# Four graph layers on one core: layer 2's sums, norms and gathers written out in a fixed order

## The chip, the core and the metric

The kernel runs on one core of a Trainium2 chip. The core has four compute engines that work side by side, each through its own queue of instructions: TensorE (PE in the profile; its weight loads are listed as PEld), VectorE (DVE), ScalarE (ACT) and GpSimd (POOL). SyncE (SP) issues DMA transfers; POOL issues the gathers, which are indirect DMAs. Engines wait for one another through semaphores. SBUF is the on-chip memory; PSUM holds the results of matmuls, in eight banks of 512 float32 per partition.

The metric is the device time of one execution, in microseconds (us). The kernel before took 2139.83 us, the median of three runs (2136.4 to 2140.26).

## What is computed

The input `x` holds 8 graphs (batches) of 2048 nodes with 64 features each, and one symmetric adjacency matrix `adj` with about 0.4% ones. Four layers follow, each of the form `x = layernorm(x + gnn(x, adj))`. The change concerns layer 2, and what layer 3 needs at its start. Layer 2 reads, cut to what matters:

```python
agg = jnp.einsum('ij,bjf->bif', A, x) / jnp.maximum(deg, 1.0)[None, :, None]
out = jax.nn.relu(x @ W_self + b_self + agg @ W_neigh + b_neigh)
out = (out - mean(out)) * rsqrt(var(out) + eps) * ln_gamma + ln_beta      # over the 64 features
x   = layernorm(x + out)
```

Layer 3 is attention with four heads: scores `h_n · h_m` with `h = x Wh` per head, a softmax over a node's neighbours, a mean of `h`, an output matrix `Wo`, and a second attention round. The kernel uses `x_n (Wh^T Wh) x_m` for the score, so for each head it keeps `G = Wh^T Wh`, and transposed copies of `Wh` and `Wo` (`AT`, `WoT`). The exponents are shifted by a number per head that comes from the mean score of node tile 0's nodes with themselves.

## The kernel before

Nodes are cut into 16 tiles of 128 (one node per partition); a tile holds 8 batches × 64 features = 512 float32 per partition. `X` (SBUF) is the current `x`.

**Layer 3's weights.** Ahead of layer 2 (lines 649 to 672) a loop over the four heads loads blocks `wb` and `ob` by SP, subtracts one column on DVE, makes `G` with one matmul, and transposes `wb` and `ob` on TensorE, with three DVE copies from PSUM.

**Layer 2, first part** (lines 742 to 760, the loop over `turns`). Per tile: transpose `X`, multiply by both weight matrices (L747), copy the neighbour part `y` to SBUF and to the DRAM table `ytab`, and split it into three bf16 pieces `Y` (hi, mid, lo: L753, L758, L759); the self part with its biases becomes `S` (L754); `b2`, layer 2's beta, is added to `X` in advance (L760).

**Layer 2, second part** (lines 762 to 835). The sum over neighbours is made in two ways. Tiles 0 to 8 are *dense*: 16 steps of 3 matmuls each (L828) over `ET`, the adjacency in fp8, and the three pieces of `Y`. Tiles 15 down to 9 go *by list*: for each of three slots POOL issues four gathers of rows of `ytab` (`fetch`, L186), and four matmuls of 32 columns (L814, with a 0/1 selection matrix copied by ACT at L810) add them up. Such a group of one tile and slot is called a quad here; there are 21. They are spread over the dense steps by `LATE` and `EARLY`, and the gathers run two quads ahead.

`finish` (L775) follows a tile's sum:

```python
STT zf = zf * r_deg + S          # L779, DVE, in PSUM
Relu on zf                       # L780, ACT, in PSUM
layer_norm(zs)                   # DVE L137-L143, ACT L151
z *= g2 ; X = z + X              # L786, L787, DVE
layer_norm(X)                    # DVE, ACT L151
Xo = X ; xtab row block <- Xo    # L792 ACT, L793 SP
```

A norm is four `bn_stats` (L137), a chain of twelve small DVE instructions for one over the root of the variance (L121 to L143, a Newton iteration), and eight activations on ACT per tile, one per batch, with scale and bias from an SBUF column (L151). `mates` joins two tiles in one PSUM tile of two banks (three such buffers) and norms them together: 9 groups, so 18 of these chains. A PSUM tile stays occupied until both tiles' z has been added to `X`.

After tile 0's norm, `first_nodes` transposes its rows (`turn_nodes`, copy by ACT), makes its scores with itself for four heads (L701 on TensorE, L703 on DVE), the shifts (L705 to L710), and the products of its nodes with `G` (`side`, L687 to L693).

**What orders the work.** In layer 2 the framework's scheduler picks each engine's order from priorities and its own estimates. Layer 3's loop is in a `manual_schedule`: there each engine takes its instructions in the order in which the program writes them. Layer 3 gathers rows of `xtab`, all of which must be written first.

Of the kernel before, what the change touches and what calls it, by code (L numbers as in the profile page):

```python
# [21 lines left out]
F32 = mybir.dt.float32  # L22
# [5 lines left out]
AF = mybir.ActivationFunctionType  # L28
ALU = mybir.AluOpType
# [3 lines left out]
P = 128  # L33
# [7 lines left out]
LEVEL = 15.0  # L41
# [7 lines left out]
def kernel(ctx: ExitStack, tc: tile.TileContext, ins: dict, out: bass.AP):  # L49
# [30 lines left out]
    def rows(name, src, pool):  # L80

        n = src.shape[0]
        t = pool.tile([P, n], F32, name=name)
        nc.sync.dma_start(t, src.unsqueeze(0).to_broadcast([P, n]))
        return t
# [556 lines left out]
    def misc(shape):  # L642
        return ps_m.tile(shape, F32, name="pm")

    ones_x = [hp.tile([P, B, D], F32, name=f"Xo{k}") for k in range(3)]
    for Xo in ones_x:
        nc.gpsimd.memset(Xo[:, :, 0:1], 1.0)

    G = hp.tile([P, HN, P], F32, name="G")
    AT = hp.tile([P, HN, P], F32, name="AT")  # L650
    WoT = hp.tile([P, HN, P], F32, name="WoT")
    for h in range(HN):
        wb = hp.tile([P, P], F32, name=f"wb{h % 2}")
        nc.gpsimd.memset(wb, 0.0)
        ob = hp.tile([P, P], F32, name=f"ob{h % 2}")
        nc.gpsimd.memset(ob, 0.0)
        for k in range(2):
            half = slice(k * D, (k + 1) * D)
            nc.sync.dma_start(wb[half, half], ins["L3_gnn_Wh"][h])
            nc.sync.dma_start(ob[half, half], ins["L3_gnn_Wo"][:, h * D:(h + 1) * D])  # L660
            nc.vector.tensor_scalar(wb[half, half], wb[half, half], wb[half, k * D:k * D + 1], None, op0=ALU.subtract)
        pg = misc([P, P])
        nc.tensor.matmul(pg, wb, wb, start=True, stop=True)
        nc.vector.tensor_copy(G[:, h], pg)
        pw = misc([P, P])
        nc.tensor.transpose(pw, wb, ident)
        nc.vector.tensor_copy(AT[:, h], pw)
        pw = misc([P, P])
        nc.tensor.transpose(pw, ob, ident)
        nc.vector.tensor_copy(WoT[:, h], pw)  # L670
        for k in range(2):
            nc.sync.dma_start(AT[k * D:k * D + 1, h, k * D:(k + 1) * D], ins["L3_gnn_bh"][h:h + 1, :])
    Us, xTs = {}, {}
    mean_row = f3w.tile([P, P], F32, name="mean_row")
    nc.vector.memset(mean_row, 1.0 / (B * P))
    shift = f3w.tile([P, 1], F32, name="shift")

    def turn_nodes(it, xi):
        px = misc([P, NP, P])
        for p in range(NP):  # L680
            nc.tensor.transpose(px[:, p], xi[:, p * P:(p + 1) * P], ident)
        xTs[it] = hp.tile([P, NP * P], F32, name="xT", bufs=2)
        nc.scalar.copy(xTs[it], px.rearrange("p a n -> p (a n)"))

    def side(it, h):
        pu = misc([P, NP, P])
        nc.tensor.matmul(pu, G[:, h], xTs[it], start=True, stop=True)  # L687
        if h == 0:
            Us[it] = hp.tile([P, NP, HN, P], F32, name="U", bufs=2)
        if h % 2:  # L690
            nc.vector.tensor_copy(Us[it][:, :, h], pu)
        else:
            nc.scalar.copy(Us[it][:, :, h], pu)  # L693

    def first_nodes(xi):

        turn_nodes(0, xi)
        self_ = hp.tile([P, HN], F32, name="self_")
        for h in range(HN):
            pu = misc([P, NP * P])  # L700
            nc.tensor.matmul(pu, G[:, h], xTs[0], start=True, stop=True)  # L701
            sq = hp.tile([P, NP * P], F32, name="sq")
            nc.vector.scalar_tensor_tensor(sq, pu, 1.0, xTs[0], op0=ALU.mult, op1=ALU.mult, accum_out=self_[:, h:h + 1])  # L703
        pm = misc([P, HN])
        nc.tensor.matmul(pm, mean_row, self_, start=True, stop=True)  # L705
        nc.vector.tensor_scalar(self_, pm, -1.0, LEVEL, op0=ALU.mult, op1=ALU.add)
        for h in range(HN):
            for k in range(2):
                row = slice(k * D, k * D + 1)
                nc.vector.tensor_copy(G[row, h, row], self_[row, h:h + 1])  # L710
        for h in range(HN):
            side(0, h)

    with ExitStack() as l2:
        wp = l2.enter_context(tc.tile_pool(name="l2w", bufs=1))
# [9 lines left out]
        nc.vector.tensor_tensor(bsn, bsn, bn, ALU.add)  # L725
        g2 = rows("g2", ins["L2_gnn_ln_gamma"], wp)
        b2 = rows("b2", ins["L2_gnn_ln_beta"], wp)
        r_deg = wp.tile([P, NT], F32, name="r_deg")
        nc.vector.tensor_scalar(r_deg, deg, 1.0, None, op0=ALU.max)
        nc.vector.reciprocal(r_deg, r_deg)  # L730
# [29 lines left out]
                nc.vector.tensor_tensor(X[:, t], X[:, t], over(b2, [P, B, D]), ALU.add)  # L760

        gk = l2.enter_context(tc.tile_pool(name="l2g", bufs=8))
        pa = l2.enter_context(tc.tile_pool(name="l2pa", bufs=3, space=PSUM))
        sums, rss, selfs, shown = {}, {}, {}, []

        mates = [(0, 1), (2, 3), (4, 5), (6, 7), (8,), (15, 14), (13, 12), (11, 10), (9,)]
        mate = {t: m for m in mates for t in m}

        def bank(it):
            m = mate[it]  # L770
            if it == m[0]:
                sums[m] = pa.tile([P, 2, B, D], F32, name="pa")
            return sums[m][:, m.index(it)]

        def finish(it):  # L775
            m = mate[it]
            po = sums[m][:, m.index(it)]
            zf = po.rearrange("p b d -> p (b d)")
            nc.vector.scalar_tensor_tensor(zf, zf, r_deg[:, it:it + 1], S[:, it].rearrange("p b d -> p (b d)"), op0=ALU.mult, op1=ALU.add)  # L779
            nc.scalar.activation(zf, zf, AF.Relu)  # L780
            if it != m[-1]:
                return
            zs = [sums[m][:, k] for k in range(len(m))]
            layer_norm(zs, wk)
            for t, z in zip(m, zs):
                nc.vector.tensor_tensor(z, z, over(g2, [P, B, D]), ALU.mult)  # L786
                nc.vector.tensor_tensor(X[:, t], z, X[:, t], ALU.add)  # L787
            layer_norm([X[:, t] for t in m], wk)
            for t in m:
                Xo = ones_x[len(shown) % len(ones_x)]  # L790
                shown.append(t)
                nc.scalar.copy(Xo[:, :, 1:], X[:, t, :, 1:])  # L792
                nc.sync.dma_start(xtab[t * P:(t + 1) * P, :], Xo.rearrange("p b d -> p (b d)"))  # L793
                if t == 0:
                    first_nodes(Xo.rearrange("p b d -> p (b d)"))

        quads = [(it, s) for it in by_list for s in range(GS)]

        def fetch(n):
            if n < len(quads):  # L800
# [5 lines left out]
        def add_edges(n):  # L806
            it, s = quads[n]
            if s == 0:
                selfs[it] = wk.tile([P, GS, P], F32, name="self_")
                nc.scalar.activation(selfs[it], Sel[:, it], AF.Copy)  # L810
                sums[it] = bank(it)
            for g in range(NG):
                nodes = slice(g * GN, (g + 1) * GN)
                nc.tensor.matmul(sums[it][nodes].rearrange("p b d -> p (b d)"), selfs[it][:, s, nodes], rss[n][g],  # L814
                                 start=(s == 0), stop=(s == GS - 1))
            if s == GS - 1:
                finish(it)

        fetch(0)
        fetch(1)  # L820
        steps = [(it, jt) for it in by_matrix for jt in range(NT)]
        LATE, EARLY = 18, 10
        n = 0
        for k, (it, jt) in enumerate(steps):
            if jt == 0:
                sums[it] = bank(it)
            for q in range(3):
                nc.tensor.matmul(sums[it].rearrange("p b d -> p (b d)"), ET[:, jt, it * P:(it + 1) * P],  # L828
                                 Y[:, jt, q].rearrange("p a n -> p (a n)"), start=(jt == 0 and q == 0), stop=(jt == NT - 1 and q == 2))
            if jt == NT - 1:  # L830
                finish(it)
            while n < len(quads) and n * (len(steps) - LATE - EARLY) <= (k - LATE) * len(quads):
                add_edges(n)
                fetch(n + 2)
                n += 1

# [19 lines left out]
    with early, ExitStack() as heads:  # L858
# [2 lines left out]
        ps_t = heads.enter_context(tc.tile_pool(name="f3pst", bufs=1, space=PSUM))  # L861
        ps_s = heads.enter_context(tc.tile_pool(name="f3pss", bufs=2, space=PSUM))
        ps_o = heads.enter_context(tc.tile_pool(name="f3pso", bufs=1, space=PSUM))
        os, xss, xsTs, ws, pos, h2s, zs, dTs = ({} for _ in range(8))

        def load_nodes(it):
            xi = wk.tile([P, BD], F32, name="xi")
            nc.sync.dma_start(xi, xtab[it * P:(it + 1) * P, :])
            turn_nodes(it, xi)

# [104 lines left out]
        def pieces(it):  # L978
# [10 lines left out]


        beside = {
            0: lambda it: [(load_nodes, it + 1)],
            1: lambda it: [(through_w, it - 1, 0), (side, it + 1, 0)],
            2: lambda it: [(sums, it - 1), (through_wo, it - 1, 0), (through_w, it - 1, 1)],
            3: lambda it: [(through_wo, it - 1, 1), (through_w, it - 1, 2)],
# [5 lines left out]
        engines = {mybir.EngineType.PE, mybir.EngineType.Activation, mybir.EngineType.DVE, mybir.EngineType.Pool}  # L1001
        AHEAD = 6
        with tc.manual_schedule(engines=engines):
            for k in range(AHEAD):
                fetch(k)
            for k in range(2):
# [22 lines left out]
    with ExitStack() as fifth:  # L1029
# [98 lines left out]
        def take_stats(it):  # L1128
            stats[it] = norm_stats([zs[it], zs[it + 1]])
# [622 lines left out]
```

## Time and profile before

| | us |
|---|---|
| median of three runs | 2139.83 |
| the profiled execution, by the clock of the runs | 2252.29 |
| its span in the profile | 2250.5 |
| layer 2, first part, in the profile | 785.8 to 843.6 |
| layer 2, second part | 843.6 to 1068.95 |
| first gather of layer 3 | 1071.77 |
| mean granted TensorE clock | 0.775 |

Busy time of each engine in the two parts of layer 2, from windows of the trace:

| part | PE | DVE | ACT | POOL |
|---|---|---|---|---|
| first, 57.8 us | 44.01 | 45.77 | 30.97 | 30.58 |
| second, 225.35 us | 154.30 | 92.16 | 109.89 | 81.86 |

How to read it: all times in the profile are those of one execution. A row of a group names line, engine, operation, result and operands, shapes and count, then busy time with the mean duration of one, then the idle time of that engine just before, with what ended it. A row of the waits names who waited for whom: total, times, longest. Being busy less than the window doesn't say that an engine is free: where two engines hand work to each other, each is idle half of the time and the stretch is still bound by the two together.

### The profile page before, as it was taken

How to read it: one execution, taken by the hardware profiler on the slowest of the kernel's cores; microseconds unless marked ns; L12 is line 12 of the kernel's file. 1: busy time of each engine (PE TensorE's matmuls, PEld its weight loads, DVE VectorE, ACT ScalarE, POOL GpSimd, SP SyncE). 2: the span in 40 equal slices, each digit the busy share in tenths (PEclk: the TensorE clock that was granted, in tenths of full speed). 3: DMA queues.
4: the chain of work that ended last, by engine and by line, in shares of the span. 5: the costliest groups of instructions: out<-in, count | busy, mean ns of one | idle time of the engine just before them, and what ended most of it. 6: DMA issues, size and time to landing. Idle time of an engine off the chain costs nothing.

```text
span 2250.5 us, 33253 instructions
## 1 busy us (share of the span) xinstructions
PE 1637.6 (73%) x12259; PEld 909.4 (40%) x12294; DVE 1390.5 (62%) x2954; ACT 997.3 (44%) x2352; POOL 1050.1 (47%) x992
## 2 busy tenths in 40 slices
PE   3552445433899979862799998999899858878872
PEld 3541111111333363320677776777667612222220
DVE  6886587785655572435244444444444459999995
ACT  4542243438523252546344444444444324555555
POOL 0002666643645356430444444444434267777762
PEclk9855565566999999986799999999999955555555
DMA  7322666631278626441432233223322155555540
GB/s 196 134 98 82 180 183 182 182 112 57 94 264 301 221 85 177 131 123 42 123 93 81 85 101 103 74 89 101 106 70 84 54 155 161 151 157 161 160 135 21
DMA packets 127690, 287.47 MB, mean 128 GB/s; under 512 B 55680, under 2 KB 56192, under 8 KB 125440
## 3 DMA queue, kind: packets, MB, share of 16 engines
q0 software_dynamic: 64896, 217.10, 31.9%
q1 hardware_dynamic: 45984, 63.96, 8.5%
q10 hardware_dynamic: 16640, 4.20, 0.8%
q8 instruction: 99, 1.62, 0.3%
q14 instruction: 71, 0.58, 0.1%
HBM read 249.29 MB, written 35.91 MB: 127 GB/s over the span
## 4 chain that ended last, share of the span: by engine, by line
PE 39%; DVE 15%; ACT 7%; issue 7%; POOL 3%; DMA 2%; another core or an unknown queue 1%; SPq 0%; DVEq 0%; ACTq 0%; POOLq 0%
PE pscore L905 7%; PE pa L556 6%; PE po L931 5%; PE pt L890 5%; PE pm L953 3%; DVE pr L1078 3%; PE pa L828 3%; PE pm L687 2%; PE pm L962 2%; DVE w L914 2%; PE pa L608 2%; DVE st L137 2%; DVE sc L1083 2%; POOL hs L186 1%; ACT w L908 1%
## 5 line engine op out<-in xcount | busy, mean ns | idle before, releaser
L914 DVE SCALAR_TENSOR_TENSOR w<-w,Sel 128x512 f32<-128x512 f32 (+1 forms) x192 | 178.4, 956 | 257.9 <-ACT w L908 257.9
L186 POOL DMA_INDIRECT hs<-htab,src x192 | 183.8, 957 | 295.0 <-PE pe L408 203.7
L186 POOL DMA_INDIRECT xs<-xtab,src x192 | 200.1, 1042 | 133.5 <-DMA xtab<-Xo 63.4
L556 PE MATMUL pa<-R,ET 128*128 128x512 bf16 x841 | 197.0, 388 | 52.5 <-POOL R L544 34.2
L905 PEld LDWEIGHTS pscore<-U,xsT 64*128 64x128 f32 x3072 | 193.9, 198 | 82.2 <-issue 82.1
L151 ACT ACTIVATE X<-X,ln_m,ln_r 128x64 f32<-128x64 f32 x384 | 131.3, 427 | 204.2 <-DVE ln_m L143 75.0
L905 PE MATMUL pscore<-U,xsT 64*128 64x64 f32 (+1 forms) x3072 | 216.4, 290 | 0.0
L908 ACT ACTIVATE w<-pscore 128x1024 f32<-128x1024 f32 x128 | 131.0, 1024 | 191.0 <-PE pscore L905 126.2
L186 POOL DMA_INDIRECT hs<-ktab,src x192 | 186.3, 970 | 55.0 <-issue 47.7
L968 POOL TENSOR_TENSOR h<-h,h2h 128x512 f32<-128x512 f32 x48 | 60.9, 1269 | 270.8 <-DVE h2h L964 270.8
L1073 PE MATMUL pe<-hi,selTb 32*128 32x512 bf16 x576 | 138.8, 619 | 52.2 <-DVE pr L1078 27.9
L890 PE MATMUL pt<-ident,xs 128*128 128x128 f32 x768 | 132.7, 298 | 44.9 <-DMA xs<-xtab,src 37.1
L892 ACT COPY xsT<-pt 128x512 f32<-128x512 f32 x192 | 112.1, 584 | 117.5 <-PE pt L890 110.7
L931 PE MATMUL po<-w,xs 128*64 128x64 f32 (+1 forms) x3072 | 147.1, 246 | 17.6 <-DVE o L936 16.5
L556 PEld LDWEIGHTS <-ET 128*128 128x128 fp8e4 x864 | 84.4, 100 | 173.9 <-issue 82.7
L931 PEld LDWEIGHTS po<-w,xs 128*64 128x64 f32 x3072 | 122.0, 140 | 35.5 <-DVE o L936 18.7
L1078 DVE TENSOR_TENSOR pr<-pe,hs 128x1024 f32<-128x1024 f32 x96 | 116.9, 1217 | 15.0 <-DMA hs<-ktab,src 10.7
L186 POOL DMA_INDIRECT rs<-ytab,src x84 | 80.4, 957 | 82.6 <-PE pa L814 52.6
L1083 DVE TENSOR_REDUCE sc<-pr 128x16 f32<-128x1024 f32 x96 | 117.1, 1219 | 2.9
L828 PE MATMUL pa<-Y,ET 128*128 128x512 bf16 x420 | 102.0, 395 | 22.5 <-DVE X L787 12.6
L890 PEld LDWEIGHTS pt<-ident,xs 128*128 128x128 f32 x768 | 85.1, 147 | 72.5 <-issue 51.7
L1085 ACT ACTIVATE w<-sc,shift 128x16 f32<-128x16 f32 x96 | 29.3, 306 | 191.3 <-DVE sc L1083 146.5
(567 smaller groups left out, 3331.9 us busy)
## 6 DMA issues: line engine op xcount, KB each, us to landing
at<-in_adj SPq DMA_DIRECT2D x16, 1024.0 KB
rtab<-r SPq DMA_DIRECT2D x16, 512.0 KB
ptab<-hp SPq DMA_DIRECT2D x16, 384.0 KB
hi<-ptab SPq DMA_DIRECT2D x16, 384.0 KB
X<-in_x ACTq DMA_DIRECT2D x16, 256.0 KB
htab<-H SPq DMA_DIRECT2D x16, 256.0 KB
ytab<-y SPq DMA_DIRECT2D x16, 256.0 KB
xtab<-Xo SPq DMA_DIRECT2D x16, 256.0 KB
```

The source lines that it names most:

```text
L151: nc.scalar.activation(v[:, b], v[:, b], AF.Identity, scale=rstd[:, k:k + 1], bias=nmr[:, k:k + 1])
L186: nc.gpsimd.indirect_dma_start(out=dst, out_offset=None, in_=table[:, :], in_offset=bass.IndirectOffsetOnAxis(ap=src[:, it, s, g:g + 1], a ...
L556: nc.tensor.matmul(po[h].rearrange("p a f -> p (a f)"), ET[:, jt, it * P:(it + 1) * P], R[:, jt, q, h].rearrange("p a f -> p (a f)"), star ...
L828: nc.tensor.matmul(sums[it].rearrange("p b d -> p (b d)"), ET[:, jt, it * P:(it + 1) * P], Y[:, jt, q].rearrange("p a n -> p (a n)"), star ...
L890: nc.tensor.transpose(pt[:, p], xss[k][n][:, p * P:(p + 1) * P], ident)
L905: nc.tensor.matmul(pscore[:, k_, f0:f0 + HN * ni].rearrange("p (h i) -> p h i", i=ni), xsTs[k][t][half, p], Us[it][half, p, :, i0:i0 + ni] ...
L908: nc.scalar.activation(w.rearrange("p t k a h i -> p k t (a h i)"), pscore.rearrange("p k (t m) -> p k t m", t=n), AF.Exp)
L914: nc.vector.scalar_tensor_tensor(wt, wt, 3.0e38, edge, op0=ALU.min, op1=ALU.mult)
L931: nc.tensor.matmul(po[half, p, :, i0:i0 + ni], xss[k][t][:, f0:f0 + D], ws[k][:, t, k_, p], start=(s == 0 and p == 0), stop=(last and p == ...
L1073: nc.tensor.matmul(pe[:, k].rearrange("p b d -> p (b d)"), selTb[nodes, s * P:(s + 1) * P], hi[nodes, q], start=(q == 0), stop=(q == 2))
L1078: nc.vector.tensor_tensor(pr.rearrange("p k b d -> p (k b d)"), pes[u].rearrange("p k b d -> p (k b d)"), hss[u].rearrange("p k b d -> p ( ...
L1083: nc.vector.tensor_reduce(sc, pr, AX.X, ALU.add)
```

## The change

1. *Layer 3's weights.* The loop is cut into `load_weights(h)` (memsets and DMAs, in front of layer 2's first part, one pair of blocks per head) and `prepare(h)`, called at dense steps 2, 6, 10 and 14. The two transposes share one PSUM tile.
2. *First nodes.* `turn_nodes(0)` is called at step 64 and reads its rows back from `xtab`; `own_scores(h)` at steps 72, 80, 88 and 96, its product written in place in PSUM; `set_shifts` at step 104; `side(0, h)` at the start of layer 3's manual part.
3. *Sums leave PSUM at once.* The scaled sum is written to `S` in SBUF, and the relu is a DVE max there. `pa` has four buffers of one bank; the normed z goes to `pz`, two banks.
4. *Norms over groups.* `sizes = [2, 4, 4, 3, 1, 1, 1]` in the order in which sums become complete: {0, 15}, {1, 14, 2, 3}, {13, 4, 12, 5}, {11, 6, 10}, {7}, {9}, {8}. That makes 7 groups and 14 chains.
5. *Order.* The loop of the second part is in a `manual_schedule` for PE, ACT, DVE and POOL. Selection matrices are copied two listed tiles ahead.

The diff, cut to its core:

```diff
-    for h in range(HN):
-        wb = hp.tile([P, P], F32, name=f"wb{h % 2}")
...
+    def load_weights(h):
+        wb = hp.tile([P, P], F32, name=f"wb{h}")
...
+    def prepare(h):
...
+        pw = misc([P, 2, P])
+        nc.tensor.transpose(pw[:, 0], wb, ident)
+        nc.tensor.transpose(pw[:, 1], ob, ident)
...
+    def own_scores(h):
+        pu = misc([P, NP * P])
+        nc.tensor.matmul(pu, G[:, h], xTs[0], start=True, stop=True)
+        nc.vector.scalar_tensor_tensor(pu, pu, 1.0, xTs[0], op0=ALU.mult, op1=ALU.mult, accum_out=self_sc[:, h:h + 1])
...
-        pa = l2.enter_context(tc.tile_pool(name="l2pa", bufs=3, space=PSUM))
+        pa = l2.enter_context(tc.tile_pool(name="l2pa", bufs=4, space=PSUM))
+        pz = l2.enter_context(tc.tile_pool(name="l2pz", bufs=2, space=PSUM))
-        mates = [(0, 1), (2, 3), (4, 5), (6, 7), (8,), (15, 14), (13, 12), (11, 10), (9,)]
...
+        sizes = [2, 4, 4, 3, 1, 1, 1]
         def finish(it):
-            nc.vector.scalar_tensor_tensor(zf, zf, r_deg[:, it:it + 1], S[:, it].rearrange("p b d -> p (b d)"), op0=ALU.mult, op1=ALU.add)
-            nc.scalar.activation(zf, zf, AF.Relu)
...
+            nc.vector.scalar_tensor_tensor(sf, sums.pop(it), r_deg[:, it:it + 1], sf, op0=ALU.mult, op1=ALU.add)
+            nc.vector.tensor_scalar(sf, sf, 0.0, None, op0=ALU.max)
...
+            take_stats(st, len(ts), S[:, it])
+            ts.append(it)
+            if len(ts) < sizes[0]:
+                return
...
+            stats = newton(st)
+            for k, t in enumerate(ts):
+                z = pz.tile([P, B, D], F32, name="z")
+                scaled(z, S[:, t], stats, k)
                 nc.vector.tensor_tensor(z, z, over(g2, [P, B, D]), ALU.mult)
                 nc.vector.tensor_tensor(X[:, t], z, X[:, t], ALU.add)
+                take_stats(st, k, X[:, t])
+            stats = newton(st)
+            for k, t in enumerate(ts):
+                scaled(X[:, t], X[:, t], stats, k)
                 Xo = ones_x[len(shown) % len(ones_x)]
                 nc.scalar.copy(Xo[:, :, 1:], X[:, t, :, 1:])
                 nc.sync.dma_start(xtab[t * P:(t + 1) * P, :], Xo.rearrange("p b d -> p (b d)"))
-                if t == 0:
-                    first_nodes(Xo.rearrange("p b d -> p (b d)"))
...
+        beside = {**{2 + 4 * h: (prepare, h) for h in range(HN)}, 64: (turn_nodes, 0),
+                  **{72 + 8 * h: (own_scores, h) for h in range(HN)}, 104: (set_shifts,)}
...
+        with tc.manual_schedule(engines=engines):
...
+                if jt == NT - 1:
+                    finish(it)
+                if k in beside:
+                    f, *a = beside[k]
+                    f(*a)
...
         with tc.manual_schedule(engines=engines):
+            for h in range(HN):
+                side(0, h)
```

## The prediction

> **What bounds the kernel now.** I read, in this order: the page's share of each engine, its groups of instructions, then for layer 2 alone (785 to 1085 us of the profiled span of 2250.5) the waits, a table by 20 us and the groups with their shapes. The page says that no single engine is full: TensorE is busy 73% of the whole span, and in the chain of waits layer 2's matmuls carry 3%. The change lies in layer 2, so its windows decide:
>
> ```profile
> 920.00:940.00 20.00, 19.36 (x92) 7.00 (x93) 11.19 (x48) 12.79 (x34) 8.12 (x9) 1.00 0.41 116
> ...
> 1000.00:1020.00 20.00, 10.06 (x42) 2.54 (x41) 9.79 (x56) 12.69 (x36) 3.83 (x4) 0.93 0.25 79
> 1020.00:1040.00 20.00, 13.42 (x47) 5.32 (x48) 12.07 (x63) 11.61 (x36) 0.00 (x0) 0.73 0.07 26
> 1040.00:1060.00 20.00, 0.00 (x0) 0.00 (x0) 8.57 (x40) 14.79 (x43) 0.00 (x0) 0.52 0.04 14
> ```
>
> The columns are the busy time of PE, PE's weight loads, DVE, ACT and POOL, then the granted clock, DMA share and GB/s. Early, TensorE is the bound (19.36 of 20); after 1000 it waits, and from 1040 it has nothing left: there DVE and ACT take turns on the last norms. The loop over dense and listed tiles runs from 843.6 (first matmul of L828) to 1068.95 (last row of `xtab` issued), 225.3 us. Layer 3 opens with a gather that needs that last row.
>
> ```profile
> POOL xs L186 <- DMA xtab<-Xo: 63.4, 1, 63.4
> POOL rs L186 <- PE pa L814: 52.6, 11, 22.5
> DVE pa L786 <- ACT pa L151: 40.3, 6, 10.4
> ACT pa L780 <- DVE pa L779: 30.4, 4, 10.8
> PE pa L828 <- DVE X L787: 12.6, 1, 12.6
> PEld pa L814 <- ACT pa L780: 9.2, 1, 9.2
> ```
>
> (engine, tile and line waited for: total, times, longest). The first row is the end of the layer; the last two, with others of 4.1, 8.3 and 5.2 us on ACT, are TensorE waiting for a PSUM tile that a norm still holds or for first_nodes' copy. Prices:
>
> ```profile
> L151 ACT ACTIVATE pa<-pa,ln_m,ln_r 128x64 f32<-128x64 f32 x128 | 47.2, 380 | 19.7 <-DVE ln_m L143 7.1 <-DVE pa L779 5.2 <-issue 4.4
> L151 ACT ACTIVATE X<-X,ln_m,ln_r 128x64 f32<-128x64 f32 x128 | 44.2, 427 | 32.1 <-DVE ln_m L143 19.9 <-DVE ln_t L126 7.6 <-remote 4.4
> L779 DVE SCALAR_TENSOR_TENSOR pa<-pa,r_deg,S 128x512 f32<-128x512 f32 x16 | 12.1, 757 | 52.2 <-PE pa L828 25.4 <-PE pa L814 21.4 <-remote 5.4
> L786 DVE TENSOR_TENSOR pa<-pa,g 128x512 f32<-128x512 f32 x16 | 11.2, 698 | 40.5 <-ACT pa L151 40.3
> L787 DVE TENSOR_TENSOR X<-pa,X 128x512 f32<-128x512 f32 x16 | 10.8, 682 | 0.2
> L780 ACT ACTIVATE pa<-pa 128x512 f32<-128x512 f32 x16 | 9.1, 572 | 36.4 <-DVE pa L779 30.4 <-DVE ln_v L140 5.4 <-issue 0.5
> L792 ACT COPY Xo<-X 128x504 f32<-128x504 f32 x16 | 9.0, 603 | 0.0
> ```
>
> Pitches, from the timeline: 16 X activations in 5.41 us (0.338 each), 16 of `pa` in 6.54 (0.409: each waits for the one before); 46 dense matmuls in 10.06 (0.219, so 0.656 for a step of three); a quad of L814 about 1.1; four bn_stats 1.2; one chain of 12 small DVE instructions ("Newton" below) 2.6.
>
> **What the Trainium skill says.** "TensorE: Matmul & The Clock Gate", Part 1: the queues of ScalarE, VectorE and GpSimd are strict FIFO, TensorE's only pulls weight loads ahead. So an instruction that waits holds all behind it; the trace agrees (POOL's 22.5 us for one L814). "ScalarE: Activation LUTs", What ACT_TABLE_LOAD costs: each [128,1] pointer adds about 93 ns to an activation, and it advises relu and max on VectorE under "Rules for kernel authors"; the pointer form at 64 elements is 427 ns here. "PSUM — Partial Sum Buffer", Summary: evacuate promptly; the 12.6 us wait above is what a late evacuation costs here.
>
> **The change part by part** (T = us after the loop's first matmul; before ends at 225.3).
>
> *Layer 3's weights.* Prepare leaves the stretch ahead of the loop (785.8 to 843.6) for steps 2, 6, 10, 14. Per head three PE pieces, about 1.03 us; in the loop 4 × about 1.2 = 4.8 us on PE, in front of tile 0's sum. DVE's copies (0.28 each) hide beside the matmuls. Ahead of the loop it gives back 4 us (2 to 7): the b2 rows still land behind 8 weight DMAs of 0.59 us on SP, so the loads come no sooner.
>
> *Sums leave at once.* STT 0.757 stays, now PSUM to `S`. L780's 572 ns on ACT become a DVE max, absent in the trace. "VectorE: DVE Perf Modes", tier table, gives fp32 tensor_scalar in SBUF two elements a cycle where tensor_tensor has one; 256 cycles fewer at its 0.96 GHz from the 0.69 of L787 is an estimate of 0.42 (bounds 0.3 and 0.7, an elementwise op at one element). ACT saves 9.1 us over 16 tiles, DVE pays 6.7. z's activation goes from SBUF to PSUM, not seen with two pointers: I take 0.42 each, 3.4 us per tile (3.3 to 3.6), since each still waits for its predecessor. X: 8 × 0.338 + 0.6 = 3.35. DVE per tile: 2.4 to take out (0.757 + 0.42 + 1.2), 2.5 between z and X (0.70 + 0.68 + 1.2).
>
> *Norms for up to four.* 7 groups instead of 9: {0,15}, {1,14,2,3}, {13,4,12,5}, {11,6,10}, {7}, {9}, {8}; 14 Newton chains, not 18, so 4 × 2.6 = 10.4 us off DVE. But a group of four holds ACT's queue for 4 × 3.4, a chain, then 4 × 3.35: 30 us.
>
> *The fixed order.* ACT, DVE, PE and POOL run in program order now. I walk it: PE 0.656 a step, a quad each 5.5 steps from step 18.
> - Tile 0 at T 15; {0,15} closes 28.4, out 30.6, Newton 33.2, z and X end about 45 to 50. Tile 1's take-out stands behind this, PE loses about 3 us at step 48.
> - Tile 3 (step 63) at 58.7. Out 60.8, Newton 63.5, z 77.6, DVE and Newton 82.6, X 96.1. The copy `xT` of turn_nodes(0), emitted at step 64, stands on ACT behind all of these: 96.7.
> - own_scores(0) at step 72 needs `xT`. TensorE reaches it at 67 and waits 29 us; behind it stand all dense sums and quads from step 72, and through the quads POOL's gathers.
> - 24 steps and 4 quads and own scores on: tile 5 at 121. Group three runs to 145 (ACT idle between 97 and 125).
> - set_shifts at step 104 needs own_scores(3) on DVE, which stands behind group three: 146. TensorE reached it at 130: 15 us more. Tile 10 at 155.6; group four: Newton 160, z 171, DVE and Newton 176, X 186.
> - Then {7}, {9}, {8}, one after the other: take-out of the next beside X, 12.9 each (Newton 2.6, z 3.4, DVE 2.5, Newton 2.6, X 2.8 less overlap, at least): 198, 211, 223.6.
>
> *Moved pieces.* side(0,h) goes to the start of layer 3's part: four PE pieces (2 in 1.13 us), two copies on ACT and DVE each, hidden by the last tiles' norms but for one DVE copy of 0.68. `xi` comes back from `xtab`: one DMA on SP, hidden while ACT's queue holds `xT` anyway. Three selections for lists, prefetched (0.52 each): 3.6 us on ACT as before. Gathers are 84 as before, 0.957 us each.
>
> Sum: −4 ahead, 223.6 + 0.7 − 225.3 = −1 in the loop, so −5. Against it: about 13 us of before's 225 are pauses of several engines at once (the trace's "remote": DVE 5.4, ACT 4.4 and 4.1, and slow chains at 889 to 908) that I can't attribute. My walk contains none. If they recur by half, +6.5; if wholly, +13. I take half: +2, rounded, against a profiled run of 2252.29. The three timed runs, median 2139.83, lie 112 lower; I carry the difference over unscaled: 2142.
>
> **Rivals.**
> - *A, the walk: waits take the place of waits* (the forecast): 29 and 15 us at steps 72 and 104 eat what prompt evacuation gives. −8 to +9, so 2132 to 2149. For it: the order on ACT's and DVE's queues. Against: every ACT phase is an estimate.
> - *B, faster:* no long wait at 72 and 104 decides, or before's pauses vanish wholly. At the far end TensorE alone sets the loop: 94.5 (432 × 0.219) + 23 + 4.8 + about 5 = 127, then the tail of three singles, 45: 172, which is 53 less, 2083. Nearer: pauses gone, z at 3.3, −5 − 4 − 6 from a shorter opening of layer 3 (there 10.5 us of the chain has no releaser): 2125. I take 2122 for this case.
> - *C, slower:* before's pauses belong to the profiled execution alone. Then the timed before-loop is 225.3 − 13 = 212, the walk's 224 stands against it, and the sum is −5 + 13 = +8; with z at its dear end (10 tiles in series × 0.2) +10: 2148 to 2150, and up to 2155 where TensorE loses clock after each long wait. For it: the profiled run is 112 us longer than the timed ones. Against: nothing says where those 112 lie. It decides once the pauses missing from the timed runs exceed 5 + 4.3 = 9.3 us.
> - *D, the change doesn't reach the time,* because something else opens layer 3: 2140. Against it, the first gather of layer 3 starts at 1071.77, 2.8 us after the last row of `xtab`, and waited 63.4 us for it. I give it nothing of its own.
>
> **How the numbers follow.** 0.2% of 2140 is 4.3 us, about what a measurement of this kernel can tell from no change. A has 0.45 (split 0.13 faster, 0.19 same, 0.13 slower), B 0.30 (faster), C 0.25 (0.24 slower, 0.01 same). Faster 0.43, same 0.20, slower 0.37. The range, 2108 to 2160, holds A, C and B down to 32 us of gain; it leaves out B's far end, where TensorE alone sets the loop, and a loop above 245. A's own range: 2132 to 2149.
>
> **What will show it.** In the new trace: the own-scores matmul idle for `xT` by 20 to 35 us near T 67; the shifts' matmul idle for DVE by 10 to 20 near T 130; three single groups of about 13 us at the end, with PE idle; activations S to z at 0.42 pitch. The prediction is wrong if PE's wait at step 72 is below 10 us, or if the loop lasts under 210 or over 240 us.

## The result and the profile after

The changed kernel takes 2152.7 us, the median of four runs (2148.37 to 2155.08), beside 2140.05 (2136.4 to 2142.82) for the kernel before: ratio 1.0058, 95% interval 1.0036 to 1.008. It is slower by 12.65 us. A repetition gave 1.0086 (1.007 to 1.0103). Four experiments (z_in_S, prep_ahead, pairs and skew) ran on a chip on which the kernel before took 2241 us, and all others on chips where it took 2140, so every ratio is to the kernel before beside the same run, and loop times of those four are set against one another first.

The two parts of layer 2 in the trace of after, from the end of layer 1 and from the first dense matmul (columns as in the prediction's window table):

```profile
757.10:816.70 59.60, 42.01 (x194) 33.60 (x193) 41.98 (x76) 31.44 (x64) 30.93 (x43) 0.91 0.23 79
816.70:1038.40 221.70, 138.44 (x625) 52.77 (x638) 108.14 (x397) 108.44 (x280) 81.66 (x85) 0.82 0.39 121
```

and three of its stretches, 20 us each:

```profile
893.70:913.70 20.00, 3.40 (x6) 1.26 (x7) 5.03 (x20) 14.09 (x38) 0.00 (x0) 0.50 0.23 79
...
993.70:1013.70 20.00, 3.25 (x12) 1.25 (x9) 9.52 (x44) 13.81 (x37) 0.00 (x0) 0.70 0.12 47
1013.70:1033.70 20.00, 2.49 (x3) 1.18 (x4) 11.93 (x49) 10.64 (x27) 0.00 (x0) 0.50 0.05 19
```

The first of them is new. In the middle of the loop, with nine of the sixteen sums still to do, TensorE is busy 3.4 of 20 us, its granted clock is 0.50, and POOL gathers nothing. The other two are the end: the last X of the group of three and then single tiles, in which DVE and ACT work mostly in turn (9.52 + 13.81, 11.93 + 10.64, of 20 us each), and TensorE has only the last of its dense matmuls (to 995.2) and layer 3's first side products. The waits of layer 2 in after:

```profile
ACT z L785 <- DVE l_m L774: 64.6, 6, 31.4
POOL xs L186 <- DMA xtab<-Xo: 60.2, 1, 60.2
POOL rs L186 <- PE pa L843: 58.2, 12, 30.7
DVE z L809 <- ACT z L785: 40.2, 16, 9.0
...
PE pm L700 <- ACT xT L660: 26.4, 1, 26.4
...
PE pm L705 <- DVE pm L701: 15.6, 1, 15.6
```

L700 is own_scores(0), waiting for the copy of xT; L705 is set_shifts, waiting for the last own score. POOL's longest wait for a sum's matmul grew from 22.5 to 30.7 us, because the quads stand behind L700. The waits for PSUM tiles of before (12.6 and 9.2 us) are gone. So the two waits that the change removes were replaced by two of other kinds, 42 us together. The prices:

```profile
L785 ACT ACTIVATE z<-S,l_m,l_r 128x64 f32<-128x64 f32 x128 | 51.5, 406 | 68.3 <-DVE l_m L774 64.6
L785 ACT ACTIVATE X<-X,l_m,l_r 128x64 f32<-128x64 f32 x128 | 44.1, 427 | 30.9 <-DVE l_m L774 30.9
...
L793 DVE SCALAR_TENSOR_TENSOR S<-pa,r_deg,S 128x512 f32<-128x512 f32 x16 | 11.9, 744 | 33.9 <-PE pa L863 23.0 <-PE pa L843 10.9
...
L794 DVE TENSOR_SCALAR S<-S 128x512 f32<-128x512 f32 x16 | 7.1, 441 | 0.6
```

The DVE max is 441 ns (0.42 was estimated); z's activations come 32 in 13.74 us, a pitch (start to start) of 0.43 (0.42 estimated).

### The profile page after: what moved, and what is told of

It is laid out like the page before. It is cut to its first block, busy times and chain, and to the rows that moved or that the text cites. A ratio compares the mean times of both kernels' runs of the same rounds, so it can differ in the third digit from the quotient of the medians.

```text
span 2153.2 us, 33182 instructions
## 1 busy us (share of the span) xinstructions
PE 1590.7 (74%) x12258; PEld 890.3 (41%) x12294; DVE 1402.7 (65%) x2922; ACT 997.9 (46%) x2336; POOL 1050.5 (49%) x992
## 4 chain that ended last, share of the span: by engine, by line
PE 40%; DVE 13%; ACT 10%; issue 5%; POOL 3%; DMA 2%; SPq 0%; ACTq 0%; POOLq 0%; DVEq 0%
PE pscore L947 7%; PE pa L556 6%; PE po L973 5%; PE pt L932 4%; PE pa L863 3%; PE pm L995 3%; PE pm L906 2%; PE po L1155 2%; ACT z L785 2%; PE pm L1004 2%; ACT z L151 2%; DVE pr L1122 2%; DVE w L956 2%; PE pa L608 2%; DMA hs<-ktab,src 1%
## 5 line engine op out<-in xcount | busy, mean ns | idle before, releaser
L947 PEld LDWEIGHTS pscore<-U,xsT 64*128 64x128 f32 x3072 | 183.8, 190 | 75.5 <-issue 75.4
L947 PE MATMUL pscore<-U,xsT 64*128 64x64 f32 (+1 forms) x3072 | 204.9, 280 | 0.0
L151 ACT ACTIVATE X<-X,ln_m,ln_r 128x64 f32<-128x64 f32 x256 | 87.2, 428 | 171.6 <-DVE ln_m L143 171.6
L1010 POOL TENSOR_TENSOR h<-h,h2h 128x512 f32<-128x512 f32 x48 | 60.9, 1269 | 214.4 <-DVE h2h L1006 214.4
L932 PE MATMUL pt<-ident,xs 128*128 128x128 f32 x768 | 127.8, 290 | 11.6 <-DMA xs<-xtab,src 9.7
L186 POOL DMA_INDIRECT rs<-rtab,src x84 | 79.6, 948 | 71.9 <-PE pa L608 51.8
L428 DVE TENSOR_TENSOR hs<-hs,w 128x2048 f32<-128x2048 f32 x48 | 106.7, 2277 | 0.5 <-ACT w L418 0.5
```

The lines of the kernel that those rows point to most:

```text
L151: nc.scalar.activation(v[:, b], v[:, b], AF.Identity, scale=rstd[:, k:k + 1], bias=nmr[:, k:k + 1])
L186: nc.gpsimd.indirect_dma_start(out=dst, out_offset=None, in_=table[:, :], in_offset=bass.IndirectOffsetOnAxis(ap=src[:, it, s, g:g + 1], a ...
L932: nc.tensor.transpose(pt[:, p], xss[k][n][:, p * P:(p + 1) * P], ident)
L947: nc.tensor.matmul(pscore[:, k_, f0:f0 + HN * ni].rearrange("p (h i) -> p h i", i=ni), xsTs[k][t][half, p], Us[it][half, p, :, i0:i0 + ni] ...
```

## The experiments

**before_again** has no edit.

> The kernel before, profiled once more. Theory 1 (before's pauses of several engines at once belonged to that one profiled execution, 112 us longer than its timed runs): span near 2140, the second part of layer 2 about 212 us instead of 225.3, shorter than the changed kernel's 221.7; so the whole loss of 12.6 us lies there and in the first part, 58 against 59.6. Rival (pauses belong to this kernel's scheduling in every execution): the second part lasts 220 us or more again, and the 12.6 us lie elsewhere, in layer 3's start for instance.

The span is 2137.9:

```profile
755.90:815.20 59.30, 45.34 (x211) 35.62 (x210) 45.20 (x94) 31.13 (x64) 30.72 (x43) 0.91 0.23 80
815.20:1023.50 208.30, 149.22 (x610) 52.20 (x622) 91.34 (x411) 109.72 (x297) 81.83 (x86) 0.88 0.42 128
```

The loop is 208.3 us with almost the same work as in the first profile (DVE 91.3 and 92.2, ACT 109.7 and 109.9): 17 us of pauses are missing. The wait for a PSUM tile is still there:

```profile
PE pa L828 <- DVE X L787: 12.7, 1, 12.7
```

Theory 1 holds for the time that is compared, though the pauses weren't of that one execution alone: four later profiles have them again (last section). Stage by stage, after minus before_again is: up to layer 2 +1.2, first part +0.3, loop +13.4, from the last row of `xtab` to layer 3's first exponential 0 (14.7 in both), layer 3's attention +0.9, rest −0.5; together the 15.3 us between the spans 2153.2 and 2137.9. The loss is in the loop.

**xt_early** moves one step number:

```diff
-        beside = {**{2 + 4 * h: (prepare, h) for h in range(HN)}, 64: (turn_nodes, 0),
+        beside = {**{2 + 4 * h: (prepare, h) for h in range(HN)}, 62: (turn_nodes, 0),
```

> The changed kernel with turn_nodes(0) at step 62 instead of 64, so that its ACT copy stands ahead of the group of four that closes at step 63. Theory 1 (the 26.4 us that TensorE waits for xT at step 72 decide the loop): that wait goes, tile 5 is complete about 28 us sooner, group three starts when group two ends, the loop falls from 221.7 to about 195 and the kernel from 2153 to about 2126. Rival (ACT's and DVE's work bounds the loop anyway, PE's wait is slack): the loop stays within 5 us of 221.7.

The loop took 196.5 us and the kernel 2133.78, 0.9966 of before (0.9953 to 0.9979). The wait for xT is gone, that for the shifts stays:

```profile
PE pm L705 <- DVE pm L701: 15.6, 1, 15.6
```

So 25 of the loop's 221.7 us hang on the place of one 0.58 us copy in ACT's queue: with that place changed the changed kernel is faster than before. The kernel gained less than the loop, 19 us of 25, and theory 1's 2126 was missed by 8: in the profiled execution, the longest of six, the stretch up to layer 2 is 4.8 us longer than in after and the first part 2.4 (62.0 against 59.6; see below).

**xt_early_shift_late** adds the second step number:

```diff
-                  **{72 + 8 * h: (own_scores, h) for h in range(HN)}, 104: (set_shifts,)}
+                  **{72 + 8 * h: (own_scores, h) for h in range(HN)}, 143: (set_shifts,)}
```

> As xt_early, and set_shifts at step 143 instead of 104, so TensorE no longer waits for DVE's last own score either. Theory 1: after the first wait is gone, ACT and DVE, not TensorE, set the order of the groups; PE runs through by about T 135, but the loop is the same as that of xt_early within 4 us. Rival: the second wait (15.6 us) also decides: another 10 to 15 us less than xt_early.

Loop 192.7, kernel 2129.35, ratio 0.9949 (0.9932 to 0.9965). TensorE finishes its dense matmuls 140 us after the loop's start, against 152.5 in xt_early, but the loop only gains 3.8: once the first wait is gone, the second, 15.6 us long, is nearly slack, as theory 1 has it.

**free_order** takes away the manual schedule in layer 2, and leaves sizes, buffers, max and moved pieces:

```diff
-        with tc.manual_schedule(engines=engines):
+        if True:
             fetch(0)
```

> The changed kernel without the manual schedule in layer 2: the framework's scheduler picks each engine's order, all else as after. Theory 1 (the fixed order, with four long phases on ACT's queue, costs the time): no wait of PE for xT above 10 us, loop 185 to 210, kernel 2115 to 2140. Rival (groups of four and three single groups at the end cost it, in whatever order): loop 215 to 225, kernel within 0.4% of 2153.

Loop 184.7, kernel 2120.88, ratio 0.9915 (0.9896 to 0.9934). The last dense matmul starts 127.4 us after the loop's start; then 57.3 us of norms remain:

```profile
946.40:966.40 20.00, 2.10 (x6) 0.76 (x4) 11.22 (x48) 14.00 (x40) 0.00 (x0) 0.62 0.05 20
966.40:986.40 20.00, 0.00 (x0) 0.00 (x0) 7.31 (x40) 12.07 (x33) 0.00 (x0) 0.50 0.10 39
```

Theory 1 holds. It also splits the change: in the scheduler's order, everything else is worth about 19 us of gain (2140 to 2121), and this fixed order then costs 32 (2121 to 2153).

**z_in_S** writes z in place, so ACT goes from SBUF to SBUF, and the two banks of `pz` go:

```diff
-                z = pz.tile([P, B, D], F32, name="z")
+                z = S[:, t]
```

> The changed kernel with z written back to S in SBUF instead of to a PSUM tile; order, groups and waits as after. Theory 1 (the loop is the chain of waits through ACT's queue, in which z of about 10 to 13 tiles stands in series at 0.43 us per activation, each waiting for the one before): SBUF activations run at 0.345 us, so 8 x 0.085 = 0.7 us less per tile, 7 to 9 us in all: loop about 213, kernel about 2144. Rival (z's pitch comes from the instruction, not from PSUM): no change, loop 220 to 223.

Loop 215.6, ratio 0.999 (0.9981 to 1.0) beside a before of 2241. The timeline of ACT, first z_in_S, then after, both for the first group of two tiles (start, duration, operation):

```profile
879.55 5.41 ACT L784 ACTIVATE S<-S,l_m,l_r 128x64 f32<-128x64 f32 x16 [33.41 <-DVE l_r L128]
```

```profile
848.67 6.91 ACT L785 ACTIVATE z<-S,l_m,l_r 128x64 f32<-128x64 f32 x16 [31.38 <-DVE l_m L774]
```

The pitch fell from 0.432 to 0.338 us, a little more than expected. The loop is 7.8 us shorter than that of prep_ahead (next), which is the nearest to after on the same chip; that is theory 1's 7 to 9, though prep_ahead also has the weights out of its loop.

PSUM as such isn't what makes the pitch, though. In free_order the same group's 16 activations, from `S` to PSUM, took

```profile
848.36 5.38 ACT L785 ACTIVATE z<-S,l_m,l_r 128x64 f32<-128x64 f32 x16 [5.23 <-DVE l_m L774]
```

which is 0.336 each. DVE gets these two tiles together, after the sixteenth activation, where in after it gets the first tile after eight: the scheduler lets two tiles take turns. In after's trace, 112 of the 128 activations of z wait for a semaphore that the activation just before raises, and most start 0.44 us after it; where a new tile follows another at once, its first one has no such wait and starts after 0.346 us. So the price is the wait for the predecessor in the same PSUM tile, which the scheduler's order avoids here.

**prep_ahead** calls prepare(h) after load_weights(h), ahead of the first part.

```diff
             load_weights(h)
+            prepare(h)
...
-        beside = {**{2 + 4 * h: (prepare, h) for h in range(HN)}, 64: (turn_nodes, 0),
+        beside = {64: (turn_nodes, 0),
```

> The changed kernel with prepare(h) called right after load_weights(h), ahead of layer 2's first part, as before. Theory 1 (the first part is paced by ACT, DVE and TensorE in turn, 5.45 us for two tiles, and prepare hid in its gaps): the first part stays 59 to 60.5 us, and the loop loses the pieces at steps 2 to 14, 3 to 5 us, as far as they are on its path: kernel 2148 to 2151. Rival (my prediction's term): the first part grows by 4 us, and the sum is the same within 2 us.

First part 61.1, loop 223.4, ratio 1.0032 (1.002 to 1.0044) beside a before of 2241. The first part did not grow by the 4 us that my term needs (after had 59.6 and, repeated, 60.9; on this chip z_in_S had 59.7 and pairs 60.3). That the loop gets shorter is not shown: the changed kernel itself was not measured on this chip.

**pairs** has `sizes = [2, 2, 2, 2, 2, 2, 2, 1, 1]`, all else as after.

> The changed kernel with sizes [2,2,2,2,2,2,2,1,1]: pairs instead of groups of four, fixed order and steps of the moved pieces as after. Theory 1 (what costs is how long a group holds ACT's queue in front of the xT copy and of own scores): the wait for xT at step 72 falls from 26 to about 14 us and the second from 16 to about 5; loop 200 to 212 despite 4 more Newton chains of 2.6 us; kernel 2133 to 2144. Rival (fewer Newton chains are worth more): loop 222 to 232.

Loop 209.1, ratio 0.996 (0.995 to 0.997) beside a before of 2241. The wait for xT is 20.9 us (14 were expected), that for the shifts 8.9 (5 expected); prep_ahead, with groups of four on the same chip, has 26.3 and 14.4, and a loop 14.3 us longer. In this fixed order, pairs are better than groups of four.

**free_pairs** has the same sizes in the free order.

> free_order with pairs, [2,2,2,2,2,2,2,1,1], so the sizes alone differ. Theory 1 (groups of four make DVE and ACT start late and leave a backlog): loop 170 to 182 against 184.7, ratio 0.984 to 0.991. Rival (four more Newton chains, 10.4 us of DVE, weigh more): loop 186 to 195, ratio above 0.992.

Loop 195.5, kernel 2129.39, ratio 0.9951 (0.9934 to 0.9969): the rival, half a microsecond beyond its range. Where nothing holds TensorE, pairs cost 10.8 us of loop. That this is near the 4 × 2.6 = 10.4 us of four Newton chains doesn't show that it is these. The loops cut at the last dense matmul, free_order first:

```profile
819.00:946.40 127.40, 125.61 (x600) 47.07 (x614) 63.83 (x251) 64.33 (x181) 82.48 (x86) 1.00 0.65 200
946.40:1003.70 57.30, 5.88 (x10) 1.94 (x8) 26.12 (x128) 36.94 (x100) 0.00 (x0) 0.54 0.07 25
```

```profile
817.90:949.00 131.10, 128.05 (x600) 47.52 (x614) 67.95 (x299) 56.70 (x162) 82.33 (x86) 0.99 0.62 191
949.00:1013.40 64.40, 5.90 (x10) 1.93 (x8) 25.84 (x128) 42.69 (x119) 0.00 (x0) 0.58 0.07 29
```

DVE's busy time grows by only 3.8 us in all, and 7.1 of the 10.8 us are in the tail, where ACT has 5.8 us more left to do and DVE no more than before. So the sizes cost time in the free order by what they leave for the tail as well, and the split between that and the chains stays open. Groups of four aren't wrong in themselves; in the fixed order of after they are, as they lengthen the queue in front of what TensorE needs.

**after_again** has no edit.

> The changed kernel itself, once more beside the kernel before. The kernel before took 2140 us beside some of the runs and 2241 beside others; its first profile is of the longer kind, with pauses in layer 2 (loop 225.4 against 208.3). Theory 1 (pauses come to whichever kernel runs there, the changed one too): ratio to before 1.003 to 1.008 in either case; the loop 222 where before takes 2140, 228 to 236 where it takes 2241. Rival (the changed kernel has none, or before alone suffers): ratio below 1.000 where before takes 2241.

Beside a before of 2137.88 it gave 1.0086, a loop of 221.7, and waits of 27.3 and 15.6 us. The case of a before of 2241 did not come up, so how the pauses strike the changed kernel itself wasn't seen; its variants z_in_S, prep_ahead, pairs and skew have them.

**free_z_in_S** joins the free order and z in S.

> free_order with z in S: the scheduler's order and 11 us less on ACT. Theory 1 (in the free order TensorE is done after 127 us and the last 57 are DVE's and ACT's backlog): some 5 to 10 us less than free_order's 184.7 loop, ratio to before 0.987 to 0.990. Rival (DVE bounds the backlog alone): the loop within 3 us of 184.7, ratio 0.991 to 0.993.

Loop 180.7, kernel 2114.88, ratio 0.9892 (0.9875 to 0.9908): 4 us of the loop, between the two expectations.

**skew** changes the order itself: a group's z is added to X (`add_normed`) only after DVE made the next group's statistics, and its X is scaled (`scale_x`) after the next group's z. It is not that alone: z is in S, `pa` has six banks, sizes are [2, 2, 2, 4, 2, 3, 1], turn_nodes is at step 62 and set_shifts at 135.

```diff
             stats = newton(st)
...
+            add_normed()
             for k, t in enumerate(ts):
-                z = pz.tile([P, B, D], F32, name="z")
-                scaled(z, S[:, t], stats, k)
...
+                scaled(S[:, t], S[:, t], stats, k)
+            scale_x()
+            normed_ts.append(ts)
```

> A fixed order in which the two halves of a norm are a group apart: DVE makes the next group's statistics before it adds this group's z to X, ACT scales the next z before this X; z in S; six PSUM banks for sums; sizes [2,2,2,4,2,3,1]; xT at step 62, shifts at step 135. Theory 1 (the changed loop is long because DVE and ACT alternate and hold TensorE, not because of their work: DVE about 126 us, ACT about 95, TensorE 127): loop 148 to 165, kernel 2080 to 2097. Rival (DVE's and ACT's work needs the time of the free order, 184.7): loop 180 or more.

Ratio 0.9856 (0.9827 to 0.9885) beside a before of 2241, loop 189.1: outside theory 1's range and inside the rival's (180 or more). It is the shortest loop of the four on its chip, but it doesn't decide between the two. The waits name one part of the excess: own rows needed too early (turn_nodes at step 62, while tile 0's X now comes a group later).

```profile
PE pm L658 <- DMA xi<-xtab: 8.7, 1, 8.7
```

Others are pauses such as before's (DVE's S waited 6.8 us for an unknown cause) and a tail of 40 us, in which X of a group of four stands ahead of the last groups.

**skew_b** addresses the early rows and the tail: `sizes = [1, 2, 2, 2, 2, 2, 2, 2, 1]`, turn_nodes at step 56, all else as in skew.

> skew with sizes [1,2,2,2,2,2,2,2,1] and xT at step 56: tile 0 stands in its own group, so its rows are in xtab before TensorE turns them (in skew it waited 8.7 us for them), and no group of four delays X at the end. Theory 1: the wait for xi goes, tail about 25 us after the last dense matmul instead of 40; ratio to before 0.978 to 0.984, against 0.9856 of skew. Rival (18 Newton chains instead of 14 bind DVE): tail 40 us or more, ratio 0.985 to 0.990.

Kernel 2093.56, ratio 0.9792 (0.9776 to 0.9809), loop 158.1 with 131.4 to the last dense matmul and a tail of 26.7. The wait for xi fell from 8.7 to 1.6 us. The kernel beats both others, and rules out skew's rival: DVE's and ACT's work fits into a loop of 158. How much of the distance from skew's 189.1 the new sizes and step are worth is open, as the two ran on different chips. A stretch of it in the middle, and its tail:

```profile
916.40:936.40 20.00, 19.89 (x93) 6.82 (x94) 16.30 (x65) 16.40 (x48) 14.44 (x14) 1.00 0.73 225
946.40:976.00 29.60, 7.73 (x18) 2.54 (x15) 20.99 (x89) 22.82 (x64) 0.00 (x0) 0.74 0.11 42
```

In the first row TensorE is full at full clock while DVE and ACT are at 16 of 20 each: together 32.7 us in 20, so they work beside each other, no longer in turn. This too is a fixed order, and its loop is 22.6 us shorter than free_z_in_S, the best of the scheduler's. What costs in after is not that the order is fixed, but which order it is. No run took the shift by a group alone: six banks, pairs, z in S and the steps came with it, so its own share isn't shown.

## Why the prediction was right and wrong

*The time.* 2142 was forecast with a range of 2108 to 2160; it is 2152.7. The range held it because it was wide, 52 us for a change worth 12.65. The likeliest case (A, 2132 to 2149) missed it by 4 us, and of the directions faster had the highest chance (0.43), where the kernel is slower. Rival C, slower at 2148 to 2155, given 0.25, is what happened, by C's mechanism.

*The walk through the queues* was the part that held. From the loop's start (816.7) in after:

| event | forecast | measured |
|---|---|---|
| X of {0, 15} done | 45 to 50 | 50.5 |
| z of group two done | 77.6 | 74.6 |
| xT copied | 96.7 | 93.5 |
| TensorE's wait for xT | 29 | 26.4 |
| tile 5's sum | 121 | 119.8 |
| wait for the shifts | 15 | 15.6 |
| X of group four done | 186 | 184.1 |
| {7}, {9}, {8} done | 198, 211, 223.6 | 195.7, 208.5, 221.7 |

xt_early shows that the wait for xT decides (25 us of loop), xt_early_shift_late that the other one hardly does after that (3.8), where the prediction counted both as eating the gain. The walk's end is closer than its parts: three singles at 12.9 us after 186 make 224.7, not 223.6; four bn_stats took 0.89 us in after, not 1.2; and X took 3.31 us a tile, which is what 8 × 0.338 + 0.6 gives, not 3.35. Its table of waits also names one wait twice, 9.2 for a weight load and 8.3 for the matmul that it belongs to.

*The term that failed* is the one under "Sum": "If they recur by half, +6.5". I set the walk, which contains no pauses, against a loop of 225.3 that contains them, and then filled the walk up by half of what I took out for them. The runs show the pauses in neither kernel in the time that is compared: before's loop is 208.3, not 225.3 (17 us, where I had counted 13), and after's is 221.7. The loop is therefore 13.4 us longer, not 1 shorter. The 112 us between the profiled and the timed runs, which I named under C, were the sign of it. I wrote that nothing says where they lie; before_again shows 17 of them in this loop, and the base of the sum should have been cut before anything was set against it. The walk itself was 2.6 us too long (223.6 + 0.7 against 221.7), which took back a part of this term and of the next.

*Layer 3's weights, "gives back 4 us":* wrong. The first part is 59.3 us before, and 59.6 and 60.9 after, though DVE does 3.2 us and PE 3.3 us less in it. In prep_ahead it is 61.1. The likely reading is that prepare lay in gaps (no engine is full: PE and DVE are busy 45 of 59.3 us); what paces this part was not isolated. Its length varies by 3 us where its code is the same (59.6 to 62.6, 62.0 or more in five runs), and why stays open; a gain of 1 or 2 us could hide in that, 4 could hardly.

*Sums at once, max, z, Newton chains:* the sizes of max and z were right (0.441, 0.43). The 10.4 us for four chains are neither shown nor refuted: free_order and free_pairs lie 10.8 us of loop apart, but only 3.8 us of DVE's busy time. What these parts are worth together, 19 us in free_order, was hidden by the order, as A says.

*Rival B* needed TensorE to run through. free_order shows the 127 us to the last dense matmul that B worked out (127.4), but a tail of 57 where B had 45: the group of three is still in work there (its X ends at 968.5, 22 us into the tail), and the three singles take the other 35. In skew_b, with pairs at the end and the two halves of a norm a group apart, the tail is 26.7.

*Rival D* is out: layer 3's first exponential comes 14.7 us after the last row of `xtab` in before_again, in after and in free_order, so what the loop gains or loses reaches layer 3 undiminished.

## What to carry to other kernels

In an order written by hand, an instruction costs what stands ahead of it in its engine's queue: a copy of 0.58 us behind a group's 64 activations held TensorE for 26 us. Place what another engine will need soon ahead of long phases. Where two engines hand work to each other, try a second group's work between the two halves of the first, so that both are busy; here that came with other edits, and took the loop to 158 us. Larger groups save small instructions but lengthen every queue. Before setting a hand-worked time against a profile, compare that profile's span with the timed runs.

## What the runs showed of the hardware

An activation of 128x64 with scale and bias from SBUF columns came every 0.338 us when it wrote to SBUF (z_in_S), and every 0.43 us when eight in a row wrote one tile in PSUM (after), although a single one was shorter there (406 ns against 427). It is the wait for the predecessor's semaphore that costs, and not PSUM: in free_order, in which two tiles take turns, 16 of them into PSUM came every 0.336 us.

The same kernel took 2140 us on the chips of eight experiments and 2241 on the chip of four (42 runs, 2235 to 2248). Its first profile is as long as the latter; which chip that was is not recorded. Of the 112 us between before's two profiles, 17 lie in layer 2's loop, 58 in layer 3's attention (692.6 against 634.7) and 30 ahead of layer 2. In that profile and in those of the four experiments, DVE, ACT and POOL stand for up to 13.8 us at a time without a releaser that the profile knows ("remote" in its rows). In all five the same 13 gathers ahead of layer 2 wait so; here before, then z_in_S.

```profile
POOL hs L186 <- remote: 37.0, 13, 4.6
```

```profile
POOL hs L186 <- remote: 34.5, 13, 4.3
```

The nine other traces have one such wait each, of DVE, 9.5 or 9.6 us. So where these pauses come is not left to chance; what causes them was not found, and whether it is the chip stays open too.
